# Every 68th quad's rows by SyncE, one-hots in PSUM, selection first, and the finishing step tile by tile

## The chip, the cores and the metric

The kernel runs on one core of a Trainium2 chip. A core has five engines with a queue each: TensorE (PE, with its weight loads shown apart as PEld), VectorE (DVE), ScalarE (ACT), GpSimd (POOL) and SyncE (SP). PSUM is the memory that PE writes its results to, SBUF the working memory. DMAs are issued from the queues of SP, ACT and POOL. The metric is the device time of one execution in microseconds (us). The kernel before took 4081.46 us in the median of ten runs (4079.01 to 4084.24).

## The reference

One layer of a graph network with 12500 nodes and 400000 edges; the edges are sorted by destination. Every node has 64 scalars and 32 vectors of three components (160 numbers).

```python
h_s = s @ lin1_ws * a * _inv(S_IN)
h_v = jnp.einsum('nci,cd->ndi', v, lin1_wv) * a[:, :, None] * _inv(V_IN)
hid = jax.nn.silu(edge_scalars @ fc_w1 * _inv(R))
w = hid @ fc_w2 * _inv(FC_HID)                       # 224 weights for each edge
es = h_s[edge_src]                                   # the gather: one row for each edge
ev = h_v[edge_src]
...                                                  # products of w, es, ev with edge_attr
agg_s = jax.ops.segment_sum(mid_s, edge_dst, num_segments=n) * inv_nn
agg_v = jax.ops.segment_sum(mid_v, edge_dst, num_segments=n) * inv_nn
o_s = agg_s @ lin2_ws * a * _inv(S_MID)
...                                                  # self connection, silu, gates
x = _layernorm(x + gated_output)
```

## The kernel before

**Tiles.** 128 edges are a tile, one edge per partition; there are 3125 tiles. Four tiles are a quad, and the main loop has 782 steps, one quad each (the last holds one tile). 24 tiles (six quads) are a chunk: the `es` loads of `load_chunk` (L228) bring a chunk's edge scalars, two DMAs of 384 KB. 72 tiles are a block of `ahead` (L174): `idx` holds their source indices (L184), `eat` their edge attributes (L185).

**Before the loop** `h_tab`, the table of h for all nodes (12500 rows of 160 float32, 640 bytes), is written to DRAM.

**One step of the loop (L785).** POOL gathers the quad's rows of `h_tab` with four indirect DMAs into `hg` (L427, pool `deep`, four buffers). PE computes the edge weights into `pw` (L440): a PSUM tile of 128 x 4 x 256 float32 of which 224 columns per tile are used; two buffers. DVE multiplies `pw` with `hg` to `pr` in four instructions (L450 and three of L458), and between them does what is due of other jobs (`first`, `rest`). Then `select_quad` (L498) makes the selection matrix on DVE: `oh`, the one-hot of the 16 destinations of a window (L504, from `rel` and `iota`), and `sel`, that times the four edge attributes (L507). Two steps later PE adds the quad up: `sel` transposed times `pr` into `pa` (L514). ACT copies `pa` out (L706), PE turns it (L523), and for every 16 blocks of three tiles `second` (L530) applies `lin2` (L538). Its result `os` is added into `acc` in SBUF by DVE (L546), at a place read from a register (the registers are loaded by DVE at L730, up to 16 at a time).

**Beside it**, spread over the steps: `hidden` for the next quads (PE L418, ACT L420), the self connection in pieces of 500 nodes (L686, L687; loads L680 and L682), and the `finish` jobs. A job takes four tiles of 128 finished nodes: PE turns `acc` (L572), DVE scales it to `z` (L573), ACT makes the gates (L579), then one step each for `gated` (L583, L584), `residual` (L591), `moments` (L596, L598), `root` (L602) and `norm` (L606, L608, and the output DMA L611). `xt`, the input rows for `residual`, is loaded when the job begins (L561). The last job (four tiles, the last of them partial) runs after the loop.

**Order.** `manual_schedule` (L778) keeps the written order on PE, DVE, ACT and POOL. SP is not in that list: its DMAs are placed by the framework's scheduler. Every DMA that SP issues uses one of eight semaphores in turn, and waits until the DMA that had this semaphore eight DMAs ago has landed.

Of the kernel before, what the change touches and what calls it, by code (L numbers as in the profile page):

```python
# [10 lines left out]
F32 = mybir.dt.float32  # L11
I32 = mybir.dt.int32
I16 = mybir.dt.int16
BF16 = mybir.dt.bfloat16
AF = mybir.ActivationFunctionType
OP = mybir.AluOpType
AX = mybir.AxisListType
ENG = mybir.EngineType
PSUM = bass.MemoryType.PSUM

P = 128
S = 64
V = 32
# [11 lines left out]
CT = 2 * SIDE  # L35
AHEAD = 3 * CT
NF = 4

MARGIN = 128
NO = 16  # L40
# [13 lines left out]
def gnn_kernel(  # L54
# [119 lines left out]
    def ahead(t):  # L174
        a0 = t // AHEAD * AHEAD
        if a0 not in aheads:
            n = min(AHEAD, TT - a0)
            idx = loads.tile([P, AHEAD], I32, name="idx")
            eat = loads.tile([P, AHEAD, 4], F32, name="eat")
            k = 0  # L180
            while k < n:
                g, u = divmod(a0 + k, GT)
                m = min(n - k, GT - u)
                nc.sync.dma_start(idx[:, k:k + m], src[g][:, u:u + m])  # L184
                nc.sync.dma_start(eat[:, k:k + m].rearrange("p t k -> p (t k)"),  # L185
                                  ea[g].rearrange("p t k -> p (t k)")[:, 4 * u:4 * (u + m)])
                k += m
            aheads[a0] = a0, idx, eat
        return aheads[a0]

    def index(t):
        a0, idx, _ = ahead(t)
        return idx[:, t - a0:t - a0 + 1]
# [229 lines left out]
    def gather(pool, idx):  # L423
# [5 lines left out]
                in_offset=bass.IndirectOffsetOnAxis(ap=i, axis=0))  # L429
        return hg  # L430

    def weights(psum, hid, slots):

        pw = psum.tile([P, Q, 256], F32, name="pw")
        n = len(slots)
        for t in range(0, n, 2):
            half, c = slots[t]
            m = min(2, n - t)
            assert half == 0 and all(slots[t + k] == (k, c) for k in range(m))
            nc.tensor.matmul(pw[:, t:t + m, :NWT], hid[:m * S, c * P:(c + 1) * P], w2[:m * S, :m],  # L440
                             start=True, stop=True)
        return pw
# [52 lines left out]
            sorted_eat[a0] = eas  # L495
        return sorted_eat[a0]

    def select_quad(pool, tiles):  # L498

        n = len(tiles)  # L500
        t0 = slot_of[tiles[0][0]]
        u = t0 % AHEAD
        oh = pool.tile([P, Q, W], F32, name="oh4")[:, :n]
        nc.vector.tensor_tensor(oh, rel[:, t0:t0 + n, None].to_broadcast([P, n, W]),  # L504
                                iota[:, None, :].to_broadcast([P, n, W]), op=OP.is_equal)
        sel = pool.tile([P, Q, 4, W], F32, name="sel", bufs=3)
        nc.vector.tensor_mul(  # L507
            sel[:, :n], oh[:, :, None, :].to_broadcast([P, n, 4, W]),
            by_slot(tiles[0][0])[:, u:u + n, :, None].to_broadcast([P, n, 4, W]))
        return sel  # L510
# [37 lines left out]

    def finish(fin, psum, t0, nt, p, most=NF):


        whole = nt if p == P else nt - 1
        xt = fin.tile([P, most, D], F32, name="xt", bufs=2)
        held = []
        if whole < nt:
            nc.vector.memset(xt[:, whole], 0.0)
        parts = [(slice(t0 * P, (t0 + whole) * P), slice(0, whole), P)] if whole else []
        if whole < nt:
            parts.append((slice((t0 + whole) * P, (t0 + whole) * P + p), slice(whole, nt), p))
        for nodes_of, k, n in parts:  # L560
            nc.sync.dma_start(xt[:n, k], x[nodes_of, :].rearrange("(t p) d -> p t d", p=n))  # L561

        def turn(k):
            if not held:
                held.extend(fin.tile([P, most, *shape], F32, name=name) for name, shape in (
                    ("z", [2 * V3]), ("sg", [V3]), ("y", [D]), ("st", [6]), ("mv", [2]),
                    ("rs", [])))
            z = held[0]
            c = (t0 + k) * P
            pp = psum.tile([P, 2, V3], F32, name="pp", tag="misc")  # L570
            for m in range(2):
                nc.tensor.transpose(pp[:, m], acc[:, m, c:c + P], ident[:V3, :V3])  # L572
            return lambda: nc.vector.tensor_scalar(  # L573
                z[:, k], pp.rearrange("p m c -> p (m c)"), at[:, t0 + k:t0 + k + 1], None,
                op0=OP.mult)

        def gates():
            z, sg = held[:2]
            nc.scalar.activation(sg[:, :nt], z[:, :nt, :V3], AF.Sigmoid)  # L579

        def gated():
            z, sg, y = held[:3]
            nc.vector.tensor_mul(y[:, :nt, :S], z[:, :nt, :S], sg[:, :nt, :S])  # L583
            nc.vector.tensor_mul(  # L584
                y[:, :nt, S:].rearrange("p t (c i) -> p t i c", i=3),
                z[:, :nt, V3:].rearrange("p t (i c) -> p t i c", i=3),
                sg[:, :nt, None, S:].to_broadcast([P, nt, 3, V]))

        def residual():
            y = held[2]  # L590
            nc.vector.tensor_add(y[:, :nt], y[:, :nt], xt[:, :nt])  # L591

        def moments():
            _, _, y, st, mv, _ = held
            for k in range(nt):
                nc.vector.bn_stats(st[:, k], y[:, k])  # L596
            for k in range(nt):
                nc.vector.bn_aggr(mv[:, k], st[:, k])  # L598

        def root():  # L600
            mv, rs = held[4:]
            nc.scalar.activation(rs[:, :nt], mv[:, :nt, 1], AF.Sqrt, bias=eps)  # L602

        def norm():
            _, _, y, _, mv, rs = held
            nc.vector.reciprocal(rs[:, :nt], rs[:, :nt])  # L606
            for k in range(nt):
                nc.vector.tensor_scalar(y[:, k], y[:, k], mv[:, k, 0:1], rs[:, k:k + 1],  # L608
                                        op0=OP.subtract, op1=OP.mult)
            for nodes_of, k, n in parts:  # L610
                nc.sync.dma_start(out[nodes_of, :].rearrange("(t p) d -> p t d", p=n), y[:n, k])  # L611

        return [lambda k=k: turn(k) for k in range(nt)] + [
            gates, gated, residual, moments, root, norm]
# [8 lines left out]
    with tc.tile_pool(  # L623
        name="fin", bufs=1
    ) as fin, tc.tile_pool(
        name="late", bufs=2
    ) as late, tc.tile_pool(name="edge", bufs=2) as edge, tc.tile_pool(
        name="deep", bufs=4
# [26 lines left out]
        def fetch(n):  # L655

            if n < len(steps):
                c, i, tiles = steps[n]
                if i == 0:
                    load_chunk(c)  # L660
                for t, _, _ in tiles:
                    ahead(t)

        def hide(n):

# [109 lines left out]
                    turning.extend(job[:nt])  # L775
                    doing.extend(job[nt:])

        with tc.manual_schedule(engines={ENG.PE, ENG.DVE, ENG.Activation, ENG.Pool}):  # L778
            fetch(0)
            hide(0)  # L780
            waits = []
# [3 lines left out]
            for n, (c, i, tiles) in enumerate(steps):  # L785
                if 2 <= n < 2 + ZP // 2:
                    for k in range(2):
                        clear(2 * (n - 2) + k)
                if n in checks:
                    checks[n]()  # L790
                fetch(n + 4)
                hg = gather(deep, [index(t) for t, _, _ in tiles])
                pw = weights(pw_ps, hids[c, i // 2], [(half, u - i // 2 * 4) for _, half, u in tiles])

                rest = turning.pop(0)() if turning else None
                step_on = not rest and doing.pop(0) if doing and not turning and not rest else None
                ready = []

                def first(n=n):
                    if rest:  # L800
                        rest()
                    ready.extend(add_up(n))

                pr = products(edge, pw, hg, len(tiles), [first, lambda n=n: ready.extend(add_up(n))])
                sel = select_quad(edge, tiles)
                for a in ready:
                    add(*a)
                if step_on:
                    step_on()
                begin()  # L810
                waits.append((tiles, pr, sel))
                if len(waits) > 2:
                    sum_up(n, *waits.pop(0))
                hide(n + 2)
                for blocks, in due(maps_due, n):
                    output(n, blocks)
                for j, sa in due(turns_due, n):
                    turn_blocks(n, j, sa)
                if products_due:
                    products_due.pop(0)()()  # L820
                if n % 30 == 13 and pieces:
                    products_due.extend([lambda: (lambda: None)] * 3 + self_connection(pieces.pop(0)))
# [141 lines left out]
```

## Time and profile before

| | |
|---|---|
| median of ten runs | 4081.46 us (4079.01 to 4084.24) |
| profiled execution | 4082.67 us, its span 4080.8 us |
| busy PE | 3694.3 us, 91% |
| busy DVE | 2428.4 us, 60% |
| busy ACT | 938.2 us, 23% |
| busy POOL | 3024.3 us, 74% |
| gathers (L427) | 3125, mean 966 ns |
| granted TensorE clock, mean | 0.959 |
| DMA queues | q0 (POOL) 256.20 MB, q1 (SP) 142.75 MB; 101 GB/s in the mean |

The page names a group of instructions by line, engine, operation and tiles (written tile <- read tiles), with count, busy time, mean of one, and the idle time of the engine before them with what ended it. "issue" is idle time in which the engine waited for nothing that the profile shows. Line numbers are those of the kernel before. A view of one line gives minimum, median and maximum duration in ns, and the starts of its first and last instruction. The timeline gives start, duration, engine, line, operation and tiles, and in brackets the idle time before. The windows give each engine's busy time in stretches of the span.

### The profile page before, as it was taken

The page shows a single profiled execution, that of the slowest core. Times are in us where ns is not written, and L with a number is a line of the kernel's source. Part 1 is how long each engine was busy: PE and PEld are TensorE (multiplying, and loading weights), DVE is VectorE, ACT ScalarE, POOL GpSimd, SP SyncE. Part 2 cuts the span into 40 slices and gives each one's busy share as a digit, 9 for nine tenths or more (in the row PEclk, how much of TensorE's full clock was granted, in tenths as well). Part 3 has the DMA queues.
Part 4 walks back from the last instruction along what each step waited for, and adds up shares of the span by engine and source line. Part 5 has one row for each costly group of instructions (what it writes and reads, how often), then busy time and mean ns, then how long its engine had stood idle before and what let it go on. Part 6 is the DMA issues. An engine that isn't in the chain of part 4 may idle for free. (4 is left out here: it accounts for less than half of the span.)

```text
span 4080.8 us, 47627 instructions
## 1 busy us (share of the span) xinstructions
PE 3694.3 (91%) x14291; PEld 1598.7 (39%) x14291; DVE 2428.4 (60%) x6374; ACT 938.2 (23%) x2463; POOL 3024.3 (74%) x3134
## 2 busy tenths in 40 slices
PE   5899999998999999999998999999899998999997
PEld 4333333433433433433433333344343333334343
DVE  4655665655656656656656556556655655655655
ACT  1312221221222222212212122222221221222222
POOL 2777777777777777777777777777777777777775
PEclk7999999999999999999999999999999999999999
DMA  7434334334334334334334334343343343433332
GB/s 210 112 91 101 100 96 102 101 94 104 101 90 107 100 90 107 102 90 108 96 94 107 93 97 107 96 105 97 96 104 94 100 103 93 103 100 96 99 93 57
DMA packets 241211, 411.77 MB, mean 101 GB/s; under 512 B 74200, under 2 KB 171876, under 8 KB 240820
## 3 DMA queue, kind: packets, MB, share of 16 engines
q0 software_dynamic: 150000, 256.20, 24.2%
q1 hardware_dynamic: 77666, 142.75, 14.5%
q10 hardware_dynamic: 13282, 9.69, 0.8%
q8 instruction: 119, 1.95, 0.2%
q14 instruction: 144, 1.18, 0.1%
HBM read 392.40 MB, written 16.00 MB: 100 GB/s over the span
## 5 line engine op out<-in xcount | busy, mean ns | idle before, releaser
L427 POOL DMA_INDIRECT hg<-h_tab,idx x3125 | 3019.5, 966 | 1024.2 <-issue 933.7
L440 PE MATMUL pw<-w,hid 128*128 128x448 f32 x3126 | 1387.8, 568 | 212.7 <-DVE oh L504 199.7
L450 DVE TENSOR_TENSOR pr<-pw,hg 128x512 f32<-128x512 f32 x782 | 539.5, 690 | 1494.5 <-DMA hg<-h_tab,idx 1068.7
L514 PE MATMUL pa<-pr,sel 128*64 128x416 f32 x6250 | 1308.6, 541 | 0.0
L458 DVE TENSOR_TENSOR pr<-pw,hg 128x384 f32<-128x384 f32 x2346 | 1153.0, 546 | 0.1
L440 PEld LDWEIGHTS pw<-w,hid 128*128 128x128 f32 x3126 | 560.8, 196 | 703.5 <-issue 636.6
L514 PEld LDWEIGHTS pa<-pr,sel 128*64 128x64 f32 x6250 | 389.8, 140 | 823.6 <-issue 713.4
L706 ACT COPY sa<-pa 128x416 f32<-128x416 f32 x521 | 263.1, 505 | 1497.4 <-PE pa L514 1494.8
L418 PE MATMUL ph<-es,w 128*128 128x512 f32 (+1 forms) x784 | 448.8, 655 | 16.0 <-DMA w<-in_fc_w_dram 12.2
L420 ACT ACTIVATE hid<-ph 128x512 f32<-128x512 f32 x392 | 233.5, 596 | 729.3 <-PE ph L418 728.9
L507 DVE TENSOR_TENSOR sel<-oh,eas 128x256 f32<-128x256 f32 x782 | 335.2, 429 | 42.9
L523 PEld LDWEIGHTS pt<-ident,sa 128*128 128x128 f32 x2084 | 239.7, 141 | 308.7 <-issue 253.2
L538 PE MATMUL po<-tt,l 128*96 128x256 f32 (+5 forms) x1496 | 346.1, 378 | 4.2 <-DVE z L573 2.8
L523 PE MATMUL pt<-ident,sa 128*128 128x128 f32 x2084 | 327.5, 280 | 0.9 <-DVE acc L687 0.7
L538 PEld LDWEIGHTS po<-tt,l 128*96 128x96 f32 (+1 forms) x1496 | 226.8, 162 | 141.9 <-issue 72.3
L526 ACT COPY tt<-pt 128x192 f32<-128x192 f32 x521 | 164.5, 316 | 500.4 <-PE pt L523 494.1
L418 PEld LDWEIGHTS ph<-es,w 128*128 128x128 f32 x784 | 119.1, 191 | 284.0 <-issue 228.9
L546 DVE TENSOR_TENSOR acc<-acc,os 96x32 f32 x1042 | 193.9, 186 | 24.7 <-ACT os L541 5.4
L504 DVE TENSOR_TENSOR oh<-rel,iota 128x64 f32<-128x64 int16 x782 | 168.7, 216 | 0.1
L572 PE MATMUL pp<-ident,acc 96*128 96x96 f32 x196 | 36.5, 271 | 95.7 <-DVE acc L546 78.4
L528 ACT COPY tt<-pt 128x64 f32<-128x64 f32 x521 | 117.2, 225 | 0.0
L541 ACT COPY os<-po 96x512 f32<-96x512 f32 (+2 forms) x68 | 38.3, 563 | 307.0 <-PE po L538 296.8
(77 smaller groups left out, 627.0 us busy)
## 6 DMA issues: line engine op xcount, KB each, us to landing
es<-in_es_t_dram SPq DMA_DIRECT2D x260, 384.0 KB
hg<-h_tab,idx POOLq DMA_INDIRECT x3125
h_tab<-ht ACTq DMA_DIRECT2D x6, 1280.0 KB
xt<-in_x_dram SPq DMA_DIRECT2D x23, 320.0 KB
out_dram<-y SPq DMA_DIRECT2D x23, 320.0 KB
xv<-in_xv_t_dram SPq DMA_DIRECT2D x25, 187.5 KB
xs<-in_xs_t_dram SPq DMA_DIRECT2D x25, 125.0 KB
xa<-in_xs_t_dram SPq DMA_DIRECT2D x12, 256.0 KB
```

The lines of the kernel that those rows point to most:

```text
L418: nc.tensor.matmul(ph[:k, c], w1[:k, :k], es[:k, t0 * P + c0 * P:t0 * P + c1 * P], start=True, stop=True)
L420: nc.scalar.activation(hid[:k, c], ph[:k, c], AF.Silu, scale=1.0 / math.sqrt(64))
L427: nc.gpsimd.indirect_dma_start(out=hg[:, t, :], out_offset=None, in_=h_tab, in_offset=bass.IndirectOffsetOnAxis(ap=i, axis=0))
L440: nc.tensor.matmul(pw[:, t:t + m, :NWT], hid[:m * S, c * P:(c + 1) * P], w2[:m * S, :m], start=True, stop=True)
L450: nc.vector.tensor_mul(two, pw[:, :n, :2 * S].rearrange("p t (k c) -> p t k c", k=2), hg[:, :n, None, :S].to_broadcast([P, n, 2, S]))
L458: nc.vector.tensor_mul(pr[:, :n, first:first + V3].rearrange("p t (i c) -> p t i c", i=3), pw[:, :n, None, 2 * S + k * V:2 * S + (k + 1) * ...
L507: nc.vector.tensor_mul(sel[:, :n], oh[:, :, None, :].to_broadcast([P, n, 4, W]), by_slot(tiles[0][0])[:, u:u + n, :, None].to_broadcast([P ...
L514: nc.tensor.matmul(pa[half * ROWS:(half + 1) * ROWS, :NPR], sel[:, t].rearrange("p k w -> p (k w)"), pr, start=start, stop=stop)
L523: nc.tensor.transpose(pt[:, four * P:four * P + k], sa[:k, c:c + P], ident[:k, :k])
L538: nc.tensor.matmul(po[:, k, :nb], l2[r, terms[to, part, four]], a[:, :nb], start=(n == 0), stop=(n == len(of) - 1))
L546: nc.vector.tensor_add(window, window, os[:, :, b])
L706: nc.scalar.copy(sa, pas.pop(j)[:, :NPR])
```

## The change

Four things change.

1. Own quads. Every 68th quad from 76 to 756 (eleven of them) is no longer gathered by POOL. SP fetches its rows with one DMA of 640 bytes for each of its 512 edges, into `hq`. Some 74 steps ahead SP loads the quad's source indices, each tile's into one partition (`places`); DVE multiplies them by 640; from 66 steps ahead, at every second step, SP loads 16 of these offsets into registers and issues 16 DMAs (`job` in `rows_of`), 32 such batches for a quad.
2. The one-hot `oh` is written to columns 224 to 239 of `pw`, in PSUM, and no longer to a tile of its own in SBUF.
3. `select_quad` stands before `products` in a step.
4. In `finish`, `gated` and `residual` go tile by tile for all jobs but the last.

With them SP's DMAs in the main loop are issued in written order too.

```diff
+OWN = 68
+BATCH = 16
+EVERY = 2
...
+    own = [n for n in range(OWN + 8, len(steps) - 4, OWN) if len(steps[n][2]) == Q]
+    by_bytes = h_tab.rearrange("n d -> (n d)").bitcast(U8)
+    row_bytes = 4 * D
+
+    def places(pool, n):
+
+        at_bytes = pool.tile([Q, P], I32, name="at_bytes")
+        for k, (t, _, _) in enumerate(steps[n][2]):
+            g, u = divmod(t, GT)
+            with nc.allow_non_contiguous_dma(reason="the indices of one tile"):
+                nc.sync.dma_start(at_bytes[k:k + 1], src[g][:, u:u + 1].rearrange("p u -> u p"))
+        return at_bytes
+
+    def rows_of(pool, at_bytes):
+
+        hq = pool.tile([P, Q, D], F32, name="hq", bufs=1)
+        flat_hq = hq.rearrange("p t d -> p (t d)").bitcast(U8)
+
+        def job(t, p0):
+            _, values = nc.values_load_multi_w_load_instructions(
+                at_bytes[t:t + 1, p0:p0 + BATCH], engines=[ENG.SP], min_val=0,
+                max_val=(N - 1) * row_bytes,
+                skip_runtime_bounds_check_because="every entry of src is the index of a node")
+            for p, v in enumerate(values, p0):
+                nc.sync.dma_start(flat_hq[p:p + 1, t * row_bytes:(t + 1) * row_bytes],
+                                  by_bytes[ds(v, row_bytes)][None])
+
+        return hq, [lambda t=t, p0=p0: job(t, p0) for t in range(Q) for p0 in range(0, P, BATCH)]
...
-    def select_quad(pool, tiles):
+    def select_quad(pool, tiles, pw):
...
-        oh = pool.tile([P, Q, W], F32, name="oh4")[:, :n]
+        oh = pw[:, :n, NWT:NWT + W]
...
+        spans = [(0, nt)] if t0 + nt == tiles_of_nodes else [(k, k + 1) for k in range(nt)]
...
-            nc.vector.tensor_mul(y[:, :nt, :S], z[:, :nt, :S], sg[:, :nt, :S])
-            nc.vector.tensor_mul(
-                y[:, :nt, S:].rearrange("p t (c i) -> p t i c", i=3),
-                z[:, :nt, V3:].rearrange("p t (i c) -> p t i c", i=3),
-                sg[:, :nt, None, S:].to_broadcast([P, nt, 3, V]))
+            for k, m in spans:
+                nc.vector.tensor_mul(y[:, k:m, :S], z[:, k:m, :S], sg[:, k:m, :S])
+                nc.vector.tensor_mul(
+                    y[:, k:m, S:].rearrange("p t (c i) -> p t i c", i=3),
+                    z[:, k:m, V3:].rearrange("p t (i c) -> p t i c", i=3),
+                    sg[:, k:m, None, S:].to_broadcast([P, m - k, 3, V]))
...
-            nc.vector.tensor_add(y[:, :nt], y[:, :nt], xt[:, :nt])
+            for k, m in spans:
+                nc.vector.tensor_add(y[:, k:m], y[:, k:m], xt[:, k:m])
...
+        at_of, hq_of, rows_due = {}, {}, []
+
+        def fetch_rows(n):
+
+            for m in own:
+                if n == max(1, m - OWN - 6):
+                    at_of[m] = places(mine, m)
+                if n == m - OWN + 2:
+                    nc.vector.tensor_scalar_mul(at_of[m], at_of[m], float(row_bytes))
+                    hq_of[m], jobs = rows_of(mine, at_of[m])
+                    rows_due.extend((m, job) for job in jobs)
+            if n % EVERY == 0 and rows_due:
+                rows_due.pop(0)[1]()
+            assert all(m > n for m, _ in rows_due)
...
-        with tc.manual_schedule(engines={ENG.PE, ENG.DVE, ENG.Activation, ENG.Pool}):
+        with tc.manual_schedule(engines={ENG.PE, ENG.DVE, ENG.Activation, ENG.Pool, ENG.SP}):
...
-                hg = gather(deep, [index(t) for t, _, _ in tiles])
+                fetch_rows(n)
+                hg = hq_of.pop(n) if n in own else gather(deep, [index(t) for t, _, _ in tiles])
...
+                sel = select_quad(edge, tiles, pw)
                 pr = products(edge, pw, hg, len(tiles), [first, lambda n=n: ready.extend(add_up(n))])
-                sel = select_quad(edge, tiles)
```

More of the change, by code (lines that the diff above doesn't have):

```diff
@@ L14 @@
 BF16 = mybir.dt.bfloat16
+U8 = mybir.dt.uint8
 AF = mybir.ActivationFunctionType
@@ L625, in gnn_kernel @@
     ) as fin, tc.tile_pool(
+        name="mine", bufs=2
+    ) as mine, tc.tile_pool(
         name="late", bufs=2
```

## The prediction

> **What bounds the kernel now.** I read the page's first two parts, then the groups of lines, then one line's own view (the gather's), then the timeline around single gathers, then the waits.
>
> The page: PE is busy 91% of the span, POOL 74%. That ranking misleads. The rows of the gather and of the first product are:
>
> ```profile
> L427 POOL DMA_INDIRECT hg<-h_tab,idx x3125 | 3019.5, 966 | 1024.2 <-issue 933.7
> L450 DVE TENSOR_TENSOR pr<-pw,hg 128x512 f32<-128x512 f32 x782 | 539.5, 690 | 1494.5 <-DMA hg<-h_tab,idx 1068.7
> ```
>
> POOL's busy and idle time add up to 4043.7 us of the 4080.8. The gather's own view gives its extremes and its place:
>
> ```profile
> L427 POOL DMA_INDIRECT hg<-h_tab,idx x3125: 942/946/2311, 78.0 to 4048.2; - x196
> ```
>
> The first gather starts at 78.0, the last ends at 4049.1. Of the idle time 72.6 us lie before the first; the other 951.6 over 3124 gaps are 0.305 us each, the same fixed gap every time. So POOL never waits for a buffer: from 78 to 4049 it is one closed chain of 3125 gathers, and 31.7 us of tail follow. That chain is the kernel. A clean gather costs 0.946 + 0.305 = 1.251 us; the mean 966 instead of 946 is an excess of 3125 x 0.0202 = 63 us. The timeline shows where it comes from (start, duration, engine, line):
>
> ```profile
> 175.04 0.42 DVE L507 TENSOR_TENSOR sel<-oh,eas 128x256 f32<-128x256 f32 x1
> 175.12 1.17 POOL L427 DMA_INDIRECT hg<-h_tab,idx  x1 [0.30 <-issue]
> ```
> ```profile
> 1045.01 0.81 DVE L591 TENSOR_TENSOR y<-y,xt 128x640 f32<-128x640 f32 x1
> 1045.26 1.38 POOL L427 DMA_INDIRECT hg<-h_tab,idx  x1 [0.30 <-issue]
> ```
> ```profile
> 1098.50 0.67 DVE L687 TENSOR_TENSOR acc<-acc,psc 96x500 f32<-96x500 f32 x1 [1.27 <-PE psc L686]
> 1098.62 0.95 POOL L427 DMA_INDIRECT hg<-h_tab,idx  x1 [0.30 <-issue]
> ```
>
> A gather that starts while `sel` or `y` (two SBUF inputs) is running is late by the rest of that instruction less about 0.13 us: 0.34 left gives 0.22, 0.56 left gives 0.43. A gather that starts under L687, which has 0.55 us left but reads one input from PSUM, takes its normal 0.95.
>
> PE has room, and it waits for DVE, which waits for the gathers:
>
> ```profile
> PE pw L440 <- DVE oh L504: 199.7, 92, 5.6
> PE pw L440 <- DVE pr L458: 10.2, 6, 4.2
> ```
>
> **The change, part by part.**
>
> *Gathers removed.* Own quads are 76, 144, ... 756: 11 quads, 44 gathers, 44 x 1.251 = 55 us off POOL's chain.
>
> *The one-hots in PSUM.* `sel` now reads PSUM and SBUF, so by the L687 pair it should stop delaying gathers. Two kinds of two-SBUF-input work stay: `oh` (216 ns) and the adds of L546 (186 ns), each worth at most 0.216 - 0.13 = 0.09 us to a gather. The pieces of `y` stay too: from the forms 128x256 at 416 and 128x128 at 282 ns a piece of 64 columns comes to 215, from 678 and 415 one of 96 to 283, from 816 and 486 one of 160 to 321 ns, so 0.19 us at most instead of 0.69. I take 10 us of the 63 as left, because most starts fall between such short pieces. The ends: 0 left, and 63 left (no gain, if PSUM does not free the port). I stay near the low end, since the nearest row, L687, reads PSUM in just this way. DVE's price: no row shows DVE writing PSUM; below, `oh` may cost nothing more than its 216 ns, or less; above, I allow it the 546 ns of a 384-column product, 258 us in all. DVE idles 2.0 us per quad (40% of 5.08), which hides even 0.33 us per quad.
>
> [...]
>
> *Selection before the products.* `oh` and `sel` (645 ns) move ahead of `pr`; both now wait for `pw`. Where the gather is late they run in time that DVE spends waiting; where PE is late the products end 0.65 us later. Behind them in DVE's order are the products, the adds and the finishing steps; PE needs `pr` and `sel` only two quads later, about 10 us. Cost 0; if that cover went, 0.65 x 175 quads that wait for PE, 114 us.
>
> *Tile by tile.* A job of four tiles grows from 416 + 678 + 816 to 4 x (215 + 283 + 321) ns, by 1.37 us, 33 us over 24 jobs, again in DVE's idle time. The last job, the one in the tail, keeps its whole-width form.
>
> *SyncE.* 5632 row DMAs, 352 register loads of 16 values, 44 index loads, 11 small DVE scalings. The prices:
>
> ```profile
> L380 SPq DMA_DIRECT2D l<-in_lin_wv_dram x15: 419/419/436, 87.9 to 95.8; - x15
> L730 DVEq TENSOR_LOAD <-rows x68: 535/1099/2299, 169.9 to 4061.9; - x68
> 94.40 1.82 SPq L380 DMA_DIRECT2D l<-in_lin_wv_dram x4
> ```
>
> Twenty small loads in a row, with the kernel's eight rotating semaphores, go out every 0.465 us without widening. So each lands within 8 x 0.465 = 3.7 us, and a batch of 16 costs 16 x 0.465 + 1.10 + about 0.1 = 8.6 us. A period of 68 quads holds 32 batches, 275 us; the `es` pairs (1.10 us each, 11.3 of them) 12 us, their landing (768 KB at the 229 GB/s of the stretch 0 to 78 is 3.4 us, so the slot eight DMAs later waits 0 to 2.6, I take 1.5) 17 us, the rest about 10 us: 314 us. The period after the change is 3863/782 = 4.94 x 68 = 336 us. SyncE fits with 22 us to spare. No row shows a DMA whose address is in a register and that moves one row; its bounds are 0.327 (the fastest load, L185) and 0.64 us (`es`, 0.59 plus the gap). I take 0.465, as L380 is small, repeated and under the same waits. It must not exceed 0.465 + 22/512 = 0.508. That is the weak point.
>
> [...]
>
> *SyncE in written order.* Before, loads went out as soon as a buffer was free. Now each stands at its place: `es` and `idx` four steps ahead of use, and behind up to one batch of 8.6 us; outputs wait there for DVE's norm, and everything behind them waits too. For `es` that leaves two steps, 9.9 us, before PE's L418, against 5 to 7 us for issue and landing. For `idx`: comparing L427's and L450's rows, POOL starts a quad's gathers 1.6 to 3 steps before its products. Cost taken 0; if that cover is gone, 43 index blocks x up to 2 us = 86 us.
>
> *Sum.* 55 + 53 = 108 us. The profiled execution took 4082.7 (1.9 us outside its span), 1.2 above the median of the ten; so 4082.7 - 108 = 3974 profiled, 3973 as the median, 2.7% faster.
>
> **Rivals.**
>
> *SyncE becomes the bound (slower).* Place: the row batches. Each 0.01 us over 0.508 per DMA adds 5.1 us per period, 56 us in all over 11; from 0.527 on the kernel is slower than before. At 0.56: 3973 + 290 = 4265; at 0.64 some 4710. For it: `es` issues cost 0.59. Against it: L380 at 0.42. Chance 0.19.
>
> *PE becomes the bound.* Without the 210 us of waits above, PE needs (3971 - 210)/782 = 4.81 us per quad; POOL will offer one each 4.94. Bursts (22 matmuls of `po`, 5.3 us) are carried by the four `hg` buffers: today the gather of quad n+4 starts 5.0 to 12.4 us after quad n's buffer is free. For PE to bind, the granted clock must fall from 0.96 to 0.93; a further 1% costs 38 us. The windows from 500 to 4000 hold 0.96 to 0.97, so against. With late index blocks it shares a middle case, 3990 to 4073. Chance 0.15.
>
> *The change does not do what it says.* PSUM does not free the port, while the 44 gathers go: 4081 - 55 = 4026; inside that middle range. If row landings also ate the 55 us, 4081: chance 0.03.
>
> **How the numbers follow.** Forecast (3955 to 3990) 0.63, the middle case 0.15, no change 0.03, slower 0.19. Range 3955 to 4075: below, all 63 us gone plus a few us of slack; above, the middle case. It leaves out the slower rival. Faster by over 0.2% (8 us, about what this kernel's measurement tells from no change) 0.78, within 0.03, slower 0.19.
>
> **What would show it.** After: 3081 gathers, median still 946, mean under 952, gaps 0.305, first start near 78. Right for SyncE: row DMAs near 0.42 us with 0.045 gaps, and SyncE idle at the end of each period. PE's waits for `pw` shrink to about 100 us. Wrong: POOL gaps of several us before a gather (buffers full, DVE waiting for `hq`: SyncE binds), or PE waiting at L418 for `es`; gathers still at 1.15 under `sel` (the port is held anyway).

## The result

The kernel after took 3992.9 us in the median of eight runs (3991.28 to 3998.55), the kernel before 4081.67 us in 28 runs beside them. The ratio is 0.9784, 95% interval 0.9775 to 0.9792: 89 us faster, where 108 were forecast.

### The profile page after: what moved, and what is told of

Same layout as the page of the kernel before. It is cut to its first block, busy times and chain, and to the rows that moved or that the text cites. A ratio compares the mean times of both kernels' runs of the same rounds, so it can differ in the third digit from the quotient of the medians.

```text
span 3999.3 us, 59309 instructions
## 1 busy us (share of the span) xinstructions
PE 3662.8 (92%) x14291; PEld 1593.6 (40%) x14291; DVE 2453.6 (61%) x6595; ACT 940.7 (24%) x2463; POOL 2945.9 (74%) x3090
## 5 line engine op out<-in xcount | busy, mean ns | idle before, releaser
L431 POOL DMA_INDIRECT hg<-h_tab,idx x3081 | 2941.1, 955 | 1012.6 <-issue 922.0
L473 PE MATMUL pw<-w,hid 128*128 128x448 f32 x3126 | 1368.7, 561 | 168.3 <-DVE acc L579 101.5
L491 DVE TENSOR_TENSOR pr<-pw,hg 128x384 f32<-128x384 f32 x2313 | 1136.5, 546 | 0.1
L483 DVE TENSOR_TENSOR pr<-pw,hg 128x512 f32<-128x512 f32 x771 | 528.6, 686 | 865.9 <-DMA hg<-h_tab,idx 864.2
L473 PEld LDWEIGHTS pw<-w,hid 128*128 128x128 f32 x3126 | 556.4, 195 | 649.6 <-issue 577.1
L537 DVE TENSOR_TENSOR pw<-rel,iota 128x64 f32<-128x64 int16 x782 | 178.8, 229 | 507.7 <-PE pw L473 504.7
L540 DVE TENSOR_TENSOR sel<-pw,eas 128x256 f32<-128x256 f32 x782 | 331.6, 424 | 43.7 <-ACT rs L638 0.5
L579 DVE TENSOR_TENSOR acc<-acc,os 96x32 f32 x1042 | 194.2, 186 | 25.4 <-ACT os L574 6.9
```

What stands on the lines that cost most here:

```text
L431: nc.gpsimd.indirect_dma_start(out=hg[:, t, :], out_offset=None, in_=h_tab, in_offset=bass.IndirectOffsetOnAxis(ap=i, axis=0))
L483: nc.vector.tensor_mul(two, pw[:, :n, :2 * S].rearrange("p t (k c) -> p t k c", k=2), hg[:, :n, None, :S].to_broadcast([P, n, 2, S]))
L491: nc.vector.tensor_mul(pr[:, :n, first:first + V3].rearrange("p t (i c) -> p t i c", i=3), pw[:, :n, None, 2 * S + k * V:2 * S + (k + 1) * ...
L540: nc.vector.tensor_mul(sel[:, :n], oh[:, :, None, :].to_broadcast([P, n, 4, W]), by_slot(tiles[0][0])[:, u:u + n, :, None].to_broadcast([P ...
L579: nc.vector.tensor_add(window, window, os[:, :, b])
```

## The profile after

The profiled execution of the kernel after took 4001.36 us, its span 3999.3. That is 8.5 us above the median of its runs, while the profiled execution of before was 1.2 above. Line numbers are now those of the kernel after: L431 is the gather (L427 before), L473 `pw` (L440), L483 and L491 the products (L450, L458), L537 and L540 the one-hot and `sel` (L504, L507), L579 the adds (L546), L618, L619 and L627 the pieces of `y` (L583, L584, L591).

The groups of instructions on the page, and the row DMAs from its list of DMA issues:

```profile
L431 POOL DMA_INDIRECT hg<-h_tab,idx x3081 | 2941.1, 955 | 1012.6 <-issue 922.0
L483 DVE TENSOR_TENSOR pr<-pw,hg 128x512 f32<-128x512 f32 x771 | 528.6, 686 | 865.9 <-DMA hg<-h_tab,idx 864.2
L537 DVE TENSOR_TENSOR pw<-rel,iota 128x64 f32<-128x64 int16 x782 | 178.8, 229 | 507.7 <-PE pw L473 504.7
L540 DVE TENSOR_TENSOR sel<-pw,eas 128x256 f32<-128x256 f32 x782 | 331.6, 424 | 43.7 <-ACT rs L638 0.5
hq<-h_tab SPq DMA_DIRECT2D x5632, 0.6 KB
```

The view of the gather's line (minimum, median, maximum in ns, first and last start):

```profile
L431 POOL DMA_INDIRECT hg<-h_tab,idx x3081: 942/947/2296, 78.7 to 3958.1; - x193
```

POOL is still one closed chain: 1012.6 us idle, of which 73.4 lie before the first gather, and the rest over 3080 gaps is 0.305 us each. From the first start to the last end it lasts 3880.4 us (78.7 to 3959.1), before 3971.1. So the chain is 90.7 us shorter:

- 44 gathers fewer at before's mean (0.966 + 0.305): 55.9 us.
- the mean of the others fell from 966.3 to 954.6 ns: 3081 x 11.7 ns = 36.0 us.
- the gaps grew by 0.3 ns each: -1 us.

The rest of the profiled execution gave 8.5 us back: 40.2 us follow the last gather, before 31.7. Two pieces of it can be read. The last step's `pw`, queued on PE behind the 22 matmuls of `po`, and what follows from it end some 3 us later (the last add of L579 ends 18.0 us after the last gather, before 15.3). And POOL's last instruction that waits, a drain at the end of the program, takes longer (view of the last line's own instructions, before and after):

```profile
L960 POOLq DRAIN  x3: 40/103/4238, 4075.8 to 4080.6; - x3
```
```profile
L1014 POOLq DRAIN  x3: 40/103/9302, 3989.1 to 3999.0; - x3
```

That is 5.1 us. The medians gained 89 us and the profiled executions 81; whether the tail or the chain is shorter in runs without a profile, no run shows.

PE's waits for `pw` (the view of waits: us in total, times, longest):

```profile
PE pw L473 <- DVE acc L579: 101.5, 57, 6.4
...
PE pw L473 <- DVE pw L537: 42.5, 19, 4.7
...
PE pw L473 <- DVE pr L491: 17.5, 11, 4.9
```

Together 161.5 us, before 209.9.

Two pieces of the timeline tell what still delays gathers. Under `sel`, which now reads PSUM, a gather takes its normal time:

```profile
3947.85 0.42 DVE L540 TENSOR_TENSOR sel<-pw,eas 128x256 f32<-128x256 f32 x1
3948.07 0.95 POOL L431 DMA_INDIRECT hg<-h_tab,idx  x1 [0.30 <-DVE pw L537]
```

Over the whole trace 159 gathers start under `sel` with at least 0.13 us of it left; the longest takes 959 ns. Before there were 350, with a median of 1112. The prediction's rule has an exception that it did not see: 48 of these 350 start within 44 ns of `sel`'s own start, and none of them takes more than 955 ns. One of them, in the kernel before:

```profile
4041.71 0.50 DVE L507 TENSOR_TENSOR sel<-oh,eas 128x256 f32<-128x256 f32 x1
4041.75 0.94 POOL L427 DMA_INDIRECT hg<-h_tab,idx  x1 [0.30 <-DVE oh L504]
```

So the comparison has to be made among the gathers that start later, with at least 0.15 us of `sel` left: before, all 296 take 977 to 1199 ns; after, all 122 take 942 to 959.

Under the pieces of `y` it is another matter:

```profile
546.19 0.40 DVE L579 TENSOR_TENSOR acc<-acc,os 96x32 f32 x2
546.47 2.30 POOL L431 DMA_INDIRECT hg<-h_tab,idx  x1 [0.30 <-DVE acc L579]
546.51 0.21 DVE L618 TENSOR_TENSOR y<-z,sg 128x64 f32<-128x64 f32 x1
546.65 0.28 DVE L619 TENSOR_TENSOR y<-z,sg 128x96 f32<-128x96 f32 x1
...
547.42 0.22 DVE L618 TENSOR_TENSOR y<-z,sg 128x64 f32<-128x64 f32 x1
...
547.56 0.28 DVE L619 TENSOR_TENSOR y<-z,sg 128x96 f32<-128x96 f32 x1
547.73 0.24 DVE L537 TENSOR_TENSOR pw<-rel,iota 128x64 f32<-128x64 int16 x1
```

The eight pieces follow one another without a gap, two adds ahead of them and the one-hot behind them, which still reads two SBUF tiles. This gather is late by 1.35 us. By the prediction's rule (the rest less 0.13 us) it would be late by 0.13 if the first piece alone held it, by 1.24 up to the end of the last piece (547.84), and by 1.37 up to the end of the one-hot (547.97). So the one-hot belongs to the row.

Not every row holds a gather to its end. In the kernel before:

```profile
4046.60 0.43 DVE L507 TENSOR_TENSOR sel<-oh,eas 128x256 f32<-128x256 f32 x1
4046.75 1.10 POOL L427 DMA_INDIRECT hg<-h_tab,idx  x1 [0.30 <-issue]
4046.94 0.49 DVE L591 TENSOR_TENSOR y<-y,xt 128x320 f32<-128x320 f32 x1
```

`y` starts before `sel` ends and reads two SBUF tiles, yet the gather is late by 0.15 us only, the rest of `sel` less 0.13. So it is with all 198 late gathers of the kernel before that start under a `sel` with an add of L546 right behind it. What makes the difference between these rows is not shown.

The gathers under `sel` go with its operand: with one input in PSUM the 122 are on time, with two in SBUF the 296 are late. That some strings of such instructions delay a gather to their end is what the trace of the kernel after adds. The prediction and the expectations speak of a port that is held or freed. That is a name for this lateness: the traces show which gathers are late and what DVE reads meanwhile, and nothing of what the two engines share.

## The experiments

Each kernel is compared with the kernel before on its own chip; not all ran on the same one. On some chips the kernel before takes 4066 to 4084 us at a granted clock of 0.96; on three others it takes 5039 to 5102 us at 0.88, and there POOL is not the bound: in the kernels traced there it waits over 900 us for DVE to free `hg` buffers (969 us for the one-hot in order_only, 1163 in rows_only), and DVE waits for PE and, over 1000 us in all, for something that the trace does not tell ("remote"). Ten of the twelve kernels fell on these three. Their times speak of another balance; what they show of single gathers and single DMAs can be read all the same. The kernel after itself was not run there.

**Is it POOL's chain? PE made light.**

```diff
-        hid = pool.tile([2 * S, Q * P], F32, name="hid")
+        hid = pool.tile([2 * S, Q * P], BF16, name="hid")
...
-            nc.tensor.matmul(pw[:, t:t + m, :NWT], hid[:m * S, c * P:(c + 1) * P], w2[:m * S, :m],
+            nc.tensor.matmul(pw[:, t:t + m, :NWT], hid[:m * S, c * P:(c + 1) * P], w2b[:m * S, :m],
```

On the kernel before:

> The kernel before with hid and w2 in bfloat16, so that PE's product of the weights (L444 here, 1388 us in all) takes one pass; nothing else is changed, and the weights are only as exact as bfloat16. The theory that POOL's chain bounds where the granted clock is near 0.96: 4075 to 4085 us, the same as the kernel before, with PE some 1000 us less busy. The rival that PE binds: some 200 us less than the kernel before or more. Where the granted clock of the kernel before is near 0.88 and it takes 5040 to 5100 us (the first six runs): the theory that PE's clock alone made these runs long expects this kernel back near 4081 us, a rival in which POOL or the memory is slow there expects over 4300 us.

Measured: 4064.95 us, the kernel before beside it 4066.15; ratio 0.9999 (0.9989 to 1.0008). PE is busy 3049.1 us instead of the 3694.3 of the profile before (taken on another chip). The product of the weights, there 3126 instructions of 568 ns (L440), is 1563 of 384 ns here; that is the one pass of the expectation. Two groups of its page:

```profile
L429 POOL DMA_INDIRECT hg<-h_tab,idx x3125 | 3003.1, 961 | 1025.3 <-issue 932.4
L442 PE MATMUL pw<-w2b,hid 128*128 128x448 bf16 x1563 | 467.6, 384 | 719.6 <-DVE pr L460 574.3
```

Some 645 us of PE's work are gone and about one us of the time: POOL's chain is the kernel. (Its chain lasts 3954.8 us, 16 less than in the profile before; the kernel before itself takes 15 us less on this chip than on the first, and no trace of it was kept here.) The granted clock was 0.883 here and 0.960 in the kernel before on the same chip, with the same time.

On the kernel after:

> The kernel after with hid and w2 in bfloat16 as in light_before (the weights are only as exact as bfloat16). Where the kernel before takes 4066 to 4081 us: the theory that the gathers alone made the gain expects the ratio of the kernel after, 0.978, to within 0.001; the theory that PE, closer to its limit now, cost the end of the kernel 8 us and nothing else expects 0.976; if PE had eaten all 19 us by which the forecast missed, 0.973 to 0.974. Where the kernel before takes over 5000 us (granted clock near 0.88): the theory that the PE clock alone made the change slower there expects 3970 to 4000 us, as on the other chips; the rival that the row DMAs of the own quads cost something without PE's help expects 4100 us or more.

Measured: 3997.86 us, the kernel before beside it 4084.33; ratio 0.9791 (0.9777 to 0.9804), against 0.9784 (0.9775 to 0.9792) of the kernel after. The first theory holds: its 0.978 lies in the interval, the 0.976 and the 0.973 to 0.974 of the others do not. Its chain of gathers lasts 3882.8 us (77.6 to 3960.3), that of the kernel after 3880.4. Its tail is shorter where PE was late (the last add ends 14.7 us after the last gather instead of 18.0); the drain of 9302 ns is there again. So PE did not eat the 19 us by which the forecast missed.

**The one-hots in PSUM alone.**

```diff
-        oh = pool.tile([P, Q, W], F32, name="oh4")[:, :n]
+        oh = pw[:, :n, NWT:NWT + W]
```

> The kernel before with the one-hot in PSUM columns of pw and nothing else of the change. My theory: sel with one PSUM input leaves the port to the gathers, so about 47 us of the 63 us excess go and the 12 us or so under y stay: 4030 to 4040 us, mean gather about 951 ns. Rival (PSUM does not free the port, the fall of the excess in the kernel after comes from the new place of sel): 4075 to 4082, mean near 966 ns.

> The kernel of psum_only again, on a chip where PE may not bind. There the mean gather fell to 950 ns. My theory where POOL's chain bounds: 3125 x 16 ns, 50 us less than the kernel before, so a ratio near 0.988 (4016 us where that takes 4066). Rival (the saved time turns into a wait elsewhere, for pw or a buffer): a ratio of 0.995 to 1.0.

Both ran where POOL is not the bound: 5132.71 us against 5102.02 (ratio 1.0076, 1.0049 to 1.0102), and 5095.71 against 5046.44 (1.0091, 1.0053 to 1.0129). The expected gain of time could not show there; that they are 0.8 to 0.9% slower is not explained. The gathers can be compared with those of a kernel with the one-hot in SBUF on such a chip (order_only, below). Group rows of psum_only's page (the mean of psum_2 is 948):

```profile
L431 POOL DMA_INDIRECT hg<-h_tab,idx x3125 | 2968.6, 950 | 2109.0 <-DVE pw L537 1134.0
L537 DVE TENSOR_TENSOR pw<-rel,iota 128x64 f32<-128x64 int16 x782 | 183.6, 235 | 26.8
L540 DVE TENSOR_TENSOR sel<-pw,eas 128x256 f32<-128x256 f32 x782 | 331.7, 424 | 44.2 <-DMA hg<-h_tab,idx 1.0
```

And of order_only's:

```profile
L431 POOL DMA_INDIRECT hg<-h_tab,idx x3125 | 3014.0, 964 | 1960.3 <-DVE oh L537 969.2
L537 DVE TENSOR_TENSOR oh<-rel,iota 128x64 f32<-128x64 int16 x782 | 171.1, 219 | 1.3 <-issue 1.2
L540 DVE TENSOR_TENSOR sel<-oh,eas 128x256 f32<-128x256 f32 x782 | 338.4, 433 | 42.7
```

`sel` still stands behind the products here, so the operand alone took 14 ns off the mean gather (45 us of POOL's busy time; in order_only 49.8 of 57.7 us of excess over 946 ns stand under `sel`, in psum_only 0.3). Of the gathers that start later than 44 ns into `sel` with at least 0.15 us of it left, 92 in psum_only and 104 in psum_2, none takes more than 959 ns. The rival, that the new place of `sel` does it, falls. The one-hot costs DVE 16 ns more when written to PSUM, `sel` 9 ns less when it reads it.

**Selection first, alone.** `select_quad` ahead of `products`, the rest as before.

> The kernel before with the selection ahead of the products and nothing else of the change; the one-hot stays in SBUF. My theory: where sel stands only shifts which gathers it meets, so the excess stays near 63 us and the time within 4060 to 4090 us. Rival (the place of sel, not the PSUM operand, makes the gain): sel runs while the last gather of its quad is under way and no gather starts under it, then 4030 to 4045 us.

Measured: 5119.2 us against 5102.02 (1.0043, 1.0021 to 1.0065), on the same chip as psum_only. The mean gather is 957 ns, the excess over the 25% point of its durations 40 us, where the kernels with `oh` in SBUF and `sel` at the old place have 64 to 66 by the same measure. Between the two theories: the place alone takes some of the delays away where gathers wait for DVE. It does so by moving the starts: 101 gathers start within 44 ns of `sel`'s start and are on time (81 of them after POOL had waited for a buffer), while all 88 that start later with at least 0.15 us left take 970 to 1195 ns. And the place has a price that neither theory named: the one-hot now stands right behind the adds, and 136 gathers lose 7.6 us under rows of adds and one-hot. In the kernel before, where products stand between the two, no gather is late in this way. On the other chips it was not run alone.

**Tile by tile, alone and taken out.** The one line that decides (`no_tiles` has the second form in the kernel after):

```diff
-        spans = [(0, nt)] if t0 + nt == tiles_of_nodes else [(k, k + 1) for k in range(nt)]
+        spans = [(0, nt)]
```

> The kernel before with gated and residual tile by tile and nothing else of the change. The prediction's theory: a gather under y is late by 0.19 us at most instead of 0.69, so 8 to 10 us are gained: 4070 to 4074 us. The theory from the trace of the kernel after: pieces that follow one another without a pause hold the port as one train, and the train is longer than the whole form (1.37 us more for each job), so nothing is gained or up to 8 us lost: 4080 to 4090 us, with gathers of 1.6 to 2.3 us under L618, L619 and L627.

Measured: 5096.09 us against 5102.02 (ratio 1.0, 0.9973 to 1.0028). The gathers:

```profile
L431 POOL DMA_INDIRECT hg<-h_tab,idx x3125 | 3014.6, 965 | 2046.4 <-DVE oh L537 1074.6
```

965 ns against 964 of order_only with whole forms. The part of the excess under `y` is 8.7 us in 41 gathers, in order_only 9.5 us in 40, in rows_only (whole forms, same chip as here) 11.4 in 39. In time nothing is gained, on a chip where POOL is not the bound.

> The kernel after with gated and residual whole again; the other three parts stay. The prediction's theory (tile by tile takes excess off the gathers): 4000 to 4004 us on the chip of the first comparison, 8 to 11 us above the 3992.9 of the kernel after. The theory from its trace (back-to-back pieces hold the port for the whole train, which is 1.37 us longer for each job): 3980 to 3993 us, the same or better, and no gather over 1.9 us for L618. If the granted clock of the kernel before is again near 0.88 as in the first four runs, PE binds and both theories give the kernel before plus or minus 1%.

> The kernel of no_tiles again, on a chip where PE may not bind: the kernel after with gated and residual whole. The kernel after stood at a ratio of 0.9784 to the kernel before. The prediction's theory (tile by tile takes 8 to 11 us off): 0.980 to 0.981. The theory that the train of pieces holds the port as the whole form does: 0.976 to 0.979.

Measured: 5325.76 us against 5038.86 (1.0566, 1.0522 to 1.0611), and 5346.24 against 5046.44 (1.0551, 1.0474 to 1.0628). The first expectation for such a chip, within 1% of the kernel before, was a miss, taken up below. The excess under `y` is 14.0 us (31 gathers) and 13.8 (31), in the kernel after 15.0 (41). So the split leaves it about as it was; with whole forms it lies anywhere from 4.9 us (psum_only) to 14.0, so the order of the other instructions counts for more. That the time is 5.5 to 5.7% longer than that of the kernel before says that on these chips the change without the split is a loss.

**Rows by SyncE, and the written order.** `rows_only` is the kernel before with the own quads and SyncE in written order; `order_only` has the written order alone (`own = []`).

> The kernel before with the eleven own quads and SyncE in written order alone; the one-hot stays in SBUF, the selection stays behind the products, gated and residual stay whole. My theory: POOL's chain bounds, so 44 gathers of 1.251 us go, 55 us, and the kernel takes about 4026 us (4020 to 4035). The port excess stays: the mean gather near 966 ns, clean ones 946. Rival (row landings or SyncE eat part of the gain): 4040 to 4081.

> The kernel of rows_only again, on a chip where PE may not bind. My theory where POOL's chain bounds: 44 gathers of 1.251 us less, 55 us, a ratio of 0.9865 (4011 us where the kernel before takes 4066). Rival (SyncE's written order and 5632 row DMAs cost something of their own, as the 3.6% of rows_only could mean): 0.99 to 1.04.

> The kernel before with SyncE's DMAs in written order and nothing else of the change: no own quads, one-hot in SBUF, selection behind the products, whole forms. The prediction's theory (cost 0): the time of the kernel before within 0.3%, 4070 to 4093 us where that takes 4081. Rival (loads that stand at their place come late, or the tail waits for them): 4090 to 4170 us, with PE waiting for es at L422 or POOL for idx. If the granted clock of the kernel before is again near 0.88: rows_only took 3.6% more there, and if the written order is the cause this one takes 3 to 4% more as well, if the row DMAs are the cause it takes the time of the kernel before.

Measured: rows_only 5277.91 us against 5102.02 (1.036, 1.0327 to 1.0392), rows_2 5228.08 against 5046.44 (1.0335, 1.0275 to 1.0394), order_only 5037.85 against 5038.86 (1.0002, 0.9973 to 1.003). On these chips the written order costs nothing and the rows cost 3.4 to 3.6%. Why is partly visible in SyncE's own line. In the kernel after (minimum, median, maximum in ns):

```profile
L460 SPq MOVE hq<-h_tab x5632: 29/29/38, 135.2 to 3820.1; - x195
L460 SPq DMA_DIRECT2D hq<-h_tab x5632: 222/228/372, 135.2 to 3820.2; - x195
```

In rows_2:

```profile
L460 SPq MOVE hq<-h_tab x5632: 2/29/1402, 154.2 to 5041.6; - x195
L460 SPq DMA_DIRECT2D hq<-h_tab x5632: 2/228/1409, 154.3 to 5041.7; - x195
```

Inside a batch the kernel after starts a row DMA every 0.323 us in the median, 0.367 in the mean (it waits now and then for an `es` load eight DMAs back: 139 times, 166 us in all, at most 2.8). In rows_2 the mean is 0.669: stretches run at 0.32, and others in steps of 0.7 us, even a register move of 29 ns taking 700. A batch lasts 4.9 us from its first to its last DMA in the kernel after (at most 8.3), in rows_2 up to 24.6. The rows then come late: POOL's waits that end with the landing of `hq` are 76 us in rows_2 and 56 in no_tiles, one for each own quad (3.7 us in the kernel after). PE waited only 44 us for `es` in rows_2 and 1.5 in no_tiles. Together that is less than the 176 to 300 us lost. DVE's waits that end with "remote" are 1380 us in rows_2 and 1115 in psum_2 on the same chip, so part of the loss stands there. Why stays open.

**More own quads, pieces apart.**

```diff
-OWN = 68
+OWN = 52
...
-            if n % EVERY == 0 and rows_due:
+            if rows_due and n % 3:
...
-            gates, gated, residual, moments, root, norm]
+            gates, *pieces, moments, root, norm]
```

`pieces` are the twelve instructions of `gated` and `residual` of a job, one a step.

> The kernel after with every 52nd quad fetched by SyncE (14 own quads in place of 11), a batch of 16 rows at two of three steps, and each piece of gated and residual in a step of its own. The theory that POOL still bounds: 12 more gathers go, 15 us, and some 12 us of excess under the trains of pieces, so 3966 us where the kernel after takes 3993, a ratio of 0.971 to 0.973. Rival (PE binds by now): 0.976 to 0.979, with PE waiting less than 100 us for pw and POOL waiting for buffers.

Measured: 5889.62 us against 5046.44 (1.1663, 1.1592 to 1.1733), on the chip of rows_2. What it would do where POOL binds is not known. Here it shows the first rival of the prediction at work, first in PE's waits, then in SyncE's timeline:

```profile
PE ph L422 <- DMA es<-in_es_t_dram: 576.8, 75, 21.7
```
```profile
1487.23 1.11 SPq L232 DMA_DIRECT2D es<-in_es_t_dram  x2
1489.91 43.23 SPq L460 DMA_DIRECT2D hq<-h_tab  x64
1533.20 0.47 SPq L737 DMA_DIRECT2D xs<-in_xs_t_dram  x1
1533.72 0.58 SPq L739 DMA_DIRECT2D xv<-in_xv_t_dram  x1
1534.41 1.11 SPq L232 DMA_DIRECT2D es<-in_es_t_dram  x2
```

64 row DMAs take 43 us, 0.68 each, the next `es` pair stands behind them, and PE waits up to 21.7 us for it. With the pieces apart, 68 gathers meet one, and together lose 9.3 us: 0.14 each, where in a row they lost 0.37 each (the longest 0.36, in a row with an add, a scaling and the one-hot). So the price of a piece by itself was about right; that instructions come in a row was not counted.

## Why the prediction was right, and where it was off

*What bounds the kernel.* Right. PE at 91% was no bound: 645 us of its work taken away left the time at 0.9999.

*44 gathers, 55 us.* Right: 55.9 by the trace.

*The one-hots in PSUM, 53 us.* The sign that the prediction read from `sel` and L687 was right: no gather that starts under `sel` is late any more (at most 959 ns, before up to 1199). The size was not: the mean gather fell by 36.0 us in all, to 955 ns, and not under 952 as the prediction's own sign asked. The failed step is "I take 10 us of the 63 as left, because most starts fall between such short pieces". Measured against 946 ns, 26.5 us are left: 15.0 under `y` (41 gathers; before 11.0 in 35), 5.8 under adds, one-hot and `sel` in a row (73 gathers), 4.5 spread thinly over all others, the rest before the loop. "0.19 us at most" for a piece of `y` was reckoned for a piece by itself (more52: 0.14 in the mean), but in this kernel eight or four pieces stand in a row behind two adds and ahead of the one-hot, and one gather lost 1.35 us.

*The one-hot's price on DVE.* Near the low end, as taken: 229 ns instead of 216, `sel` 424 instead of 429. In all `sel` became 3.6 us cheaper, and the rows of L537 and L540 together give 6.5 us more.

*Selection before the products, 0.* Right for DVE, whose wait moved: 507.7 us for `pw` now stand at L537, and those at the products fell from 1494.5 to 865.9. For the lateness of gathers it was put at nothing without a reason: the one-hot now stands right behind the adds and the pieces of `y`. 66 gathers lose 5.0 us under rows of adds and one-hot, before none, and 30 of the 44 rows of `y` in which a gather is late end in the one-hot too.

*Tile by tile.* On DVE it costs about what was worked out (31 us for the lines of `y`, forecast 33) and is hidden; to the gathers it brought nothing (15.0 us late under `y`, before 11.0).

*SyncE.* The price of 0.465 us was too high: 0.323 in the median, just under my low bound of 0.327, and 0.367 with its waits. So SyncE kept more room than the 22 us. The row taken as nearest was not near: L380's DMA takes 0.419 us to issue, a row DMA 0.228; which difference between the two counts, no run tells. On the three other chips the mean was 0.62 to 0.69, above my limit of 0.508, and the rows cost time there. But by the rival's price 0.67 would have cost some 900 us, and rows_2 lost 182; only more52, with more rows, shows PE waiting long for loads behind them (577 us). The 3.7 us for a landing were an estimate, eight starts of 0.465 us; no view of the traces times a single row to its landing.

*Written order, 0.* Right: order_only 1.0002 (on one of the three chips), and PE waited 4.7 us for `es` in the kernel after.

*The tail, taken as unchanged.* Off by 8.5 us in the profiled execution: 5.1 the drain, some 3 PE's last step.

*PE's waits for `pw`, about 100 us.* 161.5 instead.

*Sum.* 55 + 53 = 108 became 55.9 + 36.0 - 1 - 8.5 = 82.4 in the profiled execution (81.3 by its times), 89 in the medians. What failed most is the excess left under rows of short instructions, 17 of the 19 us between forecast and median. The median of 3992.9 lies 3 us outside the 3955 to 3990 that the prediction held likely (0.63), in the band of its middle case (0.15). That case did not happen: neither PE nor late index blocks bound, since no gap between two gathers is longer than 0.32 us. So the wide range was right there for another reason than the one given for its upper part.

*PE as the bound, from a clock of 0.93 down.* The first comparison did not come near it (0.966), and the light kernels do not test it: they ran at 0.883 and 0.886 without losing a us, but with some 640 us less of PE's work. They show that a low granted clock alone is no sign of a slow kernel: with PE busy 75 and 76% of the span instead of 91 and 92% the clock was 0.88 and 0.89 instead of 0.96 and 0.97, and the ratios were 0.9999 to the kernel before, and 0.9791 against the 0.9784 of the kernel after. Here a lower clock went with less work on PE; which of the two brings the other about, no run tells. On the three chips the clock of the kernel before is 0.88 too; the prediction's price (38 us for each 1% below 0.93) would make that some 200 us, and it takes about 1000 us longer. There PE, ACT and DVE stand still together for several us at a time, here for 10 (timeline of psum_only):

```profile
454.76 0.95 POOL L431 DMA_INDIRECT hg<-h_tab,idx  x1 [0.30 <-issue]
458.68 1.11 SPq L232 DMA_DIRECT2D es<-in_es_t_dram  x2
458.74 0.60 ACT L424 ACTIVATE hid<-ph 128x512 f32<-128x512 f32 x1 [16.94 <-remote]
458.80 0.69 DVE L483 TENSOR_TENSOR pr<-pw,hg 128x512 f32<-128x512 f32 x1 [10.08 <-remote]
...
459.39 1.12 PE L556 MATMUL pt<-ident,sa 128*128 128x128 f32 x4 [10.41 <-ACT hid L424]
```

`ph` had ended at 445.5 by the trace, in which the ends of matmuls are modelled; what released ACT 13 us later is not in it ("remote"). In the ten kernels on these chips DVE's waits that end so come to 1050 to 1430 us, about the time that the chips take longer; in before, after and the two light kernels there is none. What these chips do there was not found.

## What to carry to other kernels

Ask of every VectorE instruction with two SBUF inputs not only how long it is but in which unbroken row of such instructions it stands: under rows of short pieces, or of adds and one-hot, a gather often waited for the end of the row, under `sel` only for the end of `sel`. So look in the trace at what stands behind each, and count a new order of instructions among the things that make rows. One operand in PSUM took `sel` out at nearly no price (6.5 us of DVE's time in all). When a queue takes over work in small pieces, find its price on the chip and leave a factor of two: here it was 0.32 us on some chips and 0.67 on others, where the kernels with it took 3.4% longer and more.

## What was not expected of the hardware

- On three chips SyncE's instructions stretch in steps of 0.7 us (a 29 ns move to 700), and the kernel before takes 5039 to 5102 us instead of 4066 to 4084.
- POOL's drain at the end takes 4.24 us in all kernels with 3125 gathers, 9.30 us in all with 3081, 8.32 us with 3069. The cause is open.
- A row DMA landed before its semaphore was needed again: the view of SyncE's waits in the kernel after has none at L460 for another row, and eight starts take 2.6 us at the median step of 0.323.
- A gather that starts in the first 44 ns of a `sel` with two SBUF inputs is not late, one that starts later is (before: 48 gathers of at most 955 ns, 296 of at least 977).
- The median gather is 946 to 949 ns, and differs by 3 ns between psum_only and psum_2, the same kernel on two chips. Not explained.
